# Layer 1 of a two-layer graph network: the score column is copied into PSUM by ScalarE and VectorE adds the row term in one operation, in place of one ScalarE add per chunk

## The chip, the cores and the metric

One Trainium2 chip, one of its cores. The metric is device time in microseconds (us) of one execution of the whole program. Engines are named as the profile names them: PE is TensorE, PEld its weight loads, DVE is VectorE, ACT is ScalarE, POOL is GpSimd, SP is SyncE; a "q" behind a name (SPq, PEq) is that engine's queue or sequencer.

## What is computed

There are 4096 nodes with 512 features and one adjacency matrix of about 0.8% density. Layer 0 is a normalised graph convolution with a residual; layer 1, which the change concerns, is graph attention with a positive and a negative softmax. Cut to what matters:

```python
def _L1_gnn_ref(inp, adj, W, a, wtrans):          # inp = relu(layernorm(x))
    h = inp @ W
    Wh1 = h @ a[:F_out, :]                        # one number per row: s
    Wh2 = h @ a[F_out:, :]                        # one number per column: t
    e = leaky_relu(Wh1 + Wh2.T, 0.2)
    mask = adj > 0
    attention = softmax(where(mask, e, NEG_INF), axis=1)
    negative_attention = -softmax(where(mask, -e, NEG_INF), axis=1)
    h_prime = attention @ inp
    h_prime_negative = negative_attention @ inp
    new_h_prime = concatenate([h_prime, h_prime_negative], axis=1) @ wtrans
    return elu(new_h_prime)
# x = x + _L1_gnn_ref(...)
```

## The kernel before, in words

Layer 0 is dense and takes about the first half of the time. While it runs, the kernel makes lists of the non-zero columns of every block of rows. Layer 1 is sparse: it works only on listed columns. The function that the change touches is `weights(r)` inside `sparse_layer1()`.

**Blocks and pairs.** The 4096 rows are 64 blocks `r` of `RB` = 64 rows; two blocks that follow each other are a pair (32 pairs). One pair is begun during layer 0 by other code (`early_pair`); the other 31 pairs, 62 blocks, go through the loop at the end of `sparse_layer1()`. In that loop pair 17 is first (blocks 34 and 35), then pair 20 (blocks 40 and 41), then 18, 19 and so on.

**Lists and gathers.** For every pair GpSimd gathers rows of a table into SBUF (`gather`, L506, one indirect DMA per chunk of 128 listed columns). A gathered row (`ROW` = 644 words) holds the 512 features, the column's score `t` (at `ROW_T` = 512) and the mask bytes (from `ROW_W` = 516). A pair has three gathered parts, `g0`, `g1`, `g2`, with `CHUNKS` = (8, 7, 7) chunks; one chunk of `g1` holds the pair's own rows, and SyncE brings it (`load_own`, L520). So a pair has 21 indirect gathers for its 22 chunks. The even block of a pair uses parts 0 and 1 (15 chunks), the odd one parts 1 and 2 (14 chunks). Two sets of the three buffers alternate between pairs.

**`weights(r)`**, for each of the block's two parts of n chunks, in the kernel before:

1. ScalarE, per chunk (L1765): `z[:, c] = s + t[:, c]`, an activation Identity over 128x64 whose bias is the chunk's column of `t`. `z` is a PSUM bank of its own; `s` is the block's row of scores, in SBUF.
2. ScalarE (L1767): `y = 0.2 z`, the whole part, to SBUF.
3. VectorE (L1768): `z = max(z, y)`.
4. ScalarE (L1773): `e = exp(z)` into a second PSUM bank, and `z = exp(-z)` in place.
5. VectorE, twice (L1777): mask `e` and `z` into `p` (SBUF), the weights of the block.

After both parts VectorE sums `p` over the chunks (L1787, `total`).

**`product(r)`**: TensorE sums `total` over partitions (L580, `cs`); VectorE takes the reciprocal (L585, `rl`) and a sign (L588); TensorE multiplies `p` with the gathered features (L556, `u`, 20 or 22 chunk products in two halves of 64 columns each); ScalarE scales `u` by `rl` into `us` (L1815). `turn(r)` transposes `us` on TensorE (L595, `tp`), and ScalarE copies it out (L602, `ut`). `project1` and `finish1` multiply `ut` by `wtrans` on TensorE (L1826, `o`), one half after an odd block, the other after an even one; VectorE and ScalarE apply the elu (L1843 to L1847, `eo`, `y`), and SyncE stores the rows.

**Order.** The loop body is: product of block k, gathers for later blocks, `weights` of block k+2, turn of block k-1, projection. Each engine runs its own instructions in order. The order is made by the tile framework's scheduler when the program is built, apart from a few instructions that are pinned (`keep_in_program_order`). PSUM has eight banks, and `bank(...)` hands them out in rotation, so an operation that writes a new bank waits for the last reader of the bank's previous tile.

**`scores(s, z, t)`** (L524 to L529) is a helper that `early_pair` uses already: one VectorE addition of `t` (broadcast over the 64 rows) and `s` (broadcast over the chunks).

Of the kernel before, what the change touches and what calls it, by code (L numbers as in the profile page):

```python
# [13 lines left out]
AF = mybir.ActivationFunctionType  # L14
# [18 lines left out]
RB = 64  # L33
# [240 lines left out]
def gcn_gat_kernel(  # L274
# [26 lines left out]
    nc = tc.nc  # L301
# [30 lines left out]
    def bank(name):  # L332
        return ps.tile([P, 512], F32, tag="ps", name=name)
# [4 lines left out]
    with sbuf(name="init", bufs=1) as init:  # L338
        column = init.tile([P, P], F32, name="column")
        nc.vector.memset(column[:, 0:1], 0.0)  # L340
        n = 1
# [182 lines left out]
    def scores(s, z, t):  # L524

        n = z.shape[1]
        return nc.vector.tensor_tensor(
            z, t.to_broadcast([P, n, RB]), s.unsqueeze(1).to_broadcast([P, n, RB]), ALU.add
        )  # L529
# [77 lines left out]
    with sbuf(name="y0", bufs=1) as y_pool, sbuf(name="wa", bufs=1) as wa_pool, sbuf(name="bits", bufs=4) as bits_pool, sbuf(name="small0", bufs=4) as small, ExitStack() as rest, ExitStack() as lists:  # L607
# [525 lines left out]
        i0, n = GROUPS[0]  # L1133
# [557 lines left out]
    def sparse_layer1():  # L1691
        nonlocal verdict
        with ExitStack() as pools:
# [55 lines left out]
            def parts(r):  # L1749

                t = [gath[r // 2][r % 2 + k] for k in range(2)]
                return (t[0], 0, t[0].shape[1]), (t[1], t[0].shape[1], t[1].shape[1])

            def weights(r):

                nk = sum(CHUNKS[r % 2 : r % 2 + 2])
                most = CHUNKS[0] + CHUNKS[1]
                p = p_pool.tile([P, most, 2, 2, SB], F32, tag="p", name=f"p{r}")[:, :nk]
                s = srow[r // 8][:, r % 8 * RB : (r % 8 + 1) * RB]

                for gt, k, n in parts(r):
                    z = bank(f"z{r}_{k}")[:, : n * RB].rearrange("p (k c) -> p k c", c=RB)
                    t = gt[:, :, ROW_T : ROW_T + 1].bitcast(F32)
                    for c in range(n):
                        nc.scalar.activation(z[:, c], s, AF.Identity, bias=t[:, c])  # L1765
                    y = tmp.tile([P, n, RB], F32, tag=f"y{n}", name=f"y{r}_{k}")
                    nc.scalar.activation(y, z, AF.Copy, scale=ALPHA)  # L1767
                    nc.vector.tensor_tensor(z, z, y, ALU.max)  # L1768
                    e = bank(f"e{r}_{k}")[:, : n * RB].rearrange("p (k c) -> p k c", c=RB)
                    mask = gt[:, :, ROW_W:].bitcast(U8)[:, :, r % RPT * RB : (r % RPT + 1) * RB]  # L1770
                    four = "p k (h i) -> p k h i"
                    for g, x in ((0, e), (1, z)):
                        i = nc.scalar.activation(x, z, AF.Exp, scale=(1.0, -1.0)[g])  # L1773
                        if r in first:
                            tc.keep_in_program_order(i)
                    for g, x in ((0, e), (1, z)):
                        nc.vector.scalar_tensor_tensor(  # L1777
                            p[:, k : k + n, :, g],
                            mask.rearrange(four, h=2),
                            0.0,  # L1780
                            x.rearrange(four, h=2),
                            ALU.is_gt,
                            ALU.mult,
                        )
                total = small.tile([P, 2 * RB], F32, tag="total", name=f"total{r}", bufs=3)
                q = p.rearrange("p k h g i -> p (h g i) k")
                nc.vector.tensor_reduce(total, q, AX.X, ALU.add)  # L1787
                for k in range(n_late if r in with_late else 0):
                    q = lates[r][:, k].rearrange("p h g i -> p (h g i)")
                    nc.vector.tensor_tensor(total, total, q, ALU.add)  # L1790
                wgt[r] = (p, total)
# [105 lines left out]
            load_wt(1)  # L1897

            weights(order[0])
            turns = [end0(n, small, work) for n in range(2)]  # L1900
            keep_late()
            weights(order[1])
            for k, r in enumerate(order):
                product(r)
# [10 lines left out]
                if k + 2 < len(order):  # L1915
                    weights(order[k + 2])
                    if wanted and order[k + 2] % 8 == 7:
                        load_s(wanted.pop(0))
# [66 lines left out]
```

## Time and profile before

| what | value |
|---|---|
| time, median of 6 runs (lowest to highest) | 2015.33 us (2008.39 to 2028.07) |
| the profiled execution: its own time / span of its trace | 2018.65 / 2016.9 us |
| granted TensorE clock, mean | 0.973 |
| layer 1's steady loop, about 1100 to 1950 us | 850 us of the span |
| the pair begun early and the first blocks, 960 to 1100 us | 140 us |
| the tail, 1950 to 2017 us | 67 us |
| L1765 over all | 812 + 87 activations, 0.32 us each |

How to read it: times are microseconds from the start of the span unless marked ns. In the group rows, "x" is the count, then busy time and mean ns of one, and behind the bar the idle time of that engine just before these instructions with what ended most of it ("issue": nothing that the profile shows). A timeline row is: start, duration, engine, line, operation, output<-inputs, sizes, count, and in brackets the idle time before it. The engines' busy shares are averages over stages with different limits, so layer 1 is read from its own stretches.

### The profile page before, as it was taken

How to read it: one execution, taken by the hardware profiler on the slowest of the kernel's cores; microseconds unless marked ns; L12 is line 12 of the kernel's file. 1: busy time of each engine (PE TensorE's matmuls, PEld its weight loads, DVE VectorE, ACT ScalarE, POOL GpSimd, SP SyncE). 2: the span in 40 equal slices, each digit the busy share in tenths (PEclk: the TensorE clock that was granted, in tenths of full speed). 3: DMA queues.
4: the chain of work that ended last, by engine and by line, in shares of the span. 5: the costliest groups of instructions: out<-in, count | busy, mean ns of one | idle time of the engine just before them, and what ended most of it. 6: DMA issues, size and time to landing. Idle time of an engine off the chain costs nothing.

```text
span 2016.9 us, 24509 instructions
## 1 busy us (share of the span) xinstructions
PE 1903.4 (94%) x7708; PEld 1058.3 (52%) x7708; DVE 1273.4 (63%) x2758; ACT 938.0 (47%) x2165; POOL 825.7 (41%) x919
## 2 busy tenths in 40 slices
PE   8999999999999999999879998989889899898998
PEld 3444468888888888884423333333333333333334
DVE  6766588898889979762625654545555455554552
ACT  6777743222223222221536655655555555564651
POOL 3110000034322233305555666666666666666640
PEclk9999999999999999999789999999999899999999
DMA  9999967576858586758867878887888787877860
GB/s 373 392 329 338 322 197 246 174 249 206 263 165 270 176 252 194 243 178 302 284 223 233 283 246 279 249 285 248 284 265 286 237 254 244 269 245 244 259 191 23
DMA packets 217218, 504.33 MB, mean 250 GB/s; under 512 B 35059, under 2 KB 69395, under 8 KB 217078
## 3 DMA queue, kind: packets, MB, share of 16 engines
q0 software_dynamic: 62560, 233.71, 36.2%
q1 hardware_dynamic: 114240, 236.49, 34.6%
q10 hardware_dynamic: 40278, 32.47, 5.2%
q8 instruction: 63, 1.03, 0.2%
q14 instruction: 77, 0.63, 0.1%
HBM read 457.77 MB, written 103.45 MB: 278 GB/s over the span
## 4 chain that ended last, share of the span: by engine, by line
PE 89%; issue 6%; DMA 2%; DVE 1%; ACT 1%; another core or an unknown queue 0%; ACTq 0%; DVEq 0%; SPq 0%
PE p L1105 31%; PE u L556 30%; PE o L1826 11%; PE acc L1064 5%; PE yp L890 5%; PE q L1465 3%; PE tp L595 2%; DMA ar<-in_adj 2%; PE counts L867 1%; PE cs L1541 1%; ACT z L1765 1%; PE tx L831 1%; PE o L1860 0%; PE cs L580 0%; DVE key L429 0%
## 5 line engine op out<-in xcount | busy, mean ns | idle before, releaser
L506 POOL DMA_INDIRECT g<-table,idx x672 | 641.6, 955 | 434.9 <-issue 177.5
L556 PE MATMUL u<-g,p 128*64 128x512 f32 x2604 | 622.3, 607 | 75.7 <-issue 75.1
L556 PEld LDWEIGHTS u<-g,p 128*64 128x64 f32 x2604 | 190.2, 138 | 445.7 <-issue 434.0
L442 POOL DMA_INDIRECT ld<-lst,off x160 | 144.7, 904 | 342.7 <-DMA ld<-lst,off 143.7
L1765 ACT ACTIVATE z<-s,g 128x64 f32<-128x64 f32 x812 | 259.4, 319 | 42.1 <-issue 10.9
L1105 PE MATMUL p<-y,at 128*128 128x256 f32 x832 | 248.0, 380 | 0.0
L1105 PE MATMUL p<-y,sums 128*128 128x256 f32 x832 | 247.4, 379 | 0.0
L1105 PE MATMUL p<-t,sums 128*128 128x256 f32 x832 | 245.5, 379 | 0.6 <-issue 0.6
L1826 PE MATMUL o<-wt,ut 128*128 128x512 f32 x496 | 235.3, 619 | 6.1 <-DVE total L1787 3.0
L1768 DVE TENSOR_TENSOR z<-z,y 128x512 f32<-128x512 f32 (+1 forms) x124 | 80.4, 648 | 204.3 <-ACT y L1767 91.3
L1787 DVE TENSOR_REDUCE total<-p 128x128 f32<-128x1920 f32 (+1 forms) x62 | 207.6, 3349 | 2.1
L1105 PEld LDWEIGHTS p<-t,sums 128*128 128x128 f32 x832 | 158.0, 190 | 22.7 <-issue 1.2
L1105 PEld LDWEIGHTS p<-y,sums 128*128 128x128 f32 x832 | 158.0, 190 | 21.5
L1105 PEld LDWEIGHTS p<-y,at 128*128 128x128 f32 x832 | 157.1, 190 | 23.2 <-issue 2.2
L1777 DVE SCALAR_TENSOR_TENSOR p<-g,z 128x512 f32<-128x512 uint8 (+1 forms) x124 | 78.4, 632 | 112.0 <-ACT z L1773 102.9
L1826 PEld LDWEIGHTS o<-wt,ut 128*128 128x128 f32 x496 | 94.8, 202 | 103.4 <-issue 98.5
L852 ACT ACTIVATE junk<-ar 128x1024 bf16<-128x1024 f32 x128 | 134.6, 1051 | 9.2 <-DMA ar<-in_adj 5.0
L930 ACT ACTIVATE m<-at 128x1024 uint8<-128x1024 f32 x110 | 113.0, 1047 | 51.9 <-DVE t_all L1032 16.0
L1773 ACT ACTIVATE e<-z 128x512 f32<-128x512 f32 (+1 forms) x124 | 67.1, 542 | 128.6 <-issue 71.3
L1777 DVE SCALAR_TENSOR_TENSOR p<-g,e 128x512 f32<-128x512 uint8 (+1 forms) x124 | 79.1, 638 | 74.4 <-issue 29.8
L1105 PE MATMUL p<-t,at 128*128 128x256 f32 x416 | 123.9, 380 | 1.2 <-DVE w L975 1.2
L1064 PE MATMUL acc<-y,at 128*128 128x512 f32 x256 | 120.3, 594 | 0.0
(220 smaller groups left out, 2037.1 us busy)
## 6 DMA issues: line engine op xcount, KB each, us to landing
ar<-in_adj SPq DMA_DIRECT2D x128, 512.0 KB
at<-in_adj_t SPq DMA_DIRECT2D x112, 512.0 KB
table<-table SPq DMA_DIRECT2D x49, 1032.0 KB
table<-m ACTq DMA_DIRECT2D x48, 256.0 KB
g<-table,idx POOLq DMA_INDIRECT x672
g<-table SPq DMA_DIRECT2D x32, 322.0 KB
at<-in_adj_t SPq DMA_DIRECT2D x32, 256.0 KB
xr<-in_x SPq DMA_DIRECT2D x32, 256.0 KB
```

The source lines that it names most:

```text
L442: return nc.gpsimd.indirect_dma_start(out=lst_dram[g][e % TURNS][:, :], out_offset=bass.IndirectOffsetOnAxis(ap=off[g][:, e, c : c + 1], a ...
L506: i = nc.gpsimd.indirect_dma_start(out=gt[:, k, :], out_offset=None, in_=table[2 * n // RPT], in_offset=bass.IndirectOffsetOnAxis(ap=idx[n ...
L556: i = nc.tensor.matmul(u[h * RB : (h + 1) * RB], p[:, k, h].rearrange("p g i -> p (g i)"), row(k), start=begin and k == HALVES[r % 2][h][0 ...
L852: nc.scalar.activation(junk, ar, AF.Identity, accum_out=parts[j][:, c : c + 1])
L890: nc.tensor.matmul(yp, hx_t[j][:, c * P : (c + 1) * P], w0_sb[:, c, :], start=c == 0, stop=c == FC - 1,)
L930: nc.scalar.activation(m, at, AF.Sign)
L1064: nc.tensor.matmul(a, at[:, 0, it * P : (it + 1) * P], y0[j], start=j == 0, stop=j == NJ - 1)
L1105: i = nc.tensor.matmul(out, left[:, x * P : (x + 1) * P], right, start=jp == 0 and first, stop=jp == NP - 1 and (final or not first),)
L1765: nc.scalar.activation(z[:, c], s, AF.Identity, bias=t[:, c])
L1777: nc.vector.scalar_tensor_tensor(p[:, k : k + n, :, g], mask.rearrange(four, h=2), 0.0, x.rearrange(four, h=2), ALU.is_gt, ALU.mult,)
L1787: nc.vector.tensor_reduce(total, q, AX.X, ALU.add)
L1826: i = nc.tensor.matmul(halves[j], uts[j][:, g, c, :], wts[g][:, c, :], start=g == 0 and c == 0, stop=g == 1 and c == FC - 1,)
```

## The change

For each part, ScalarE no longer adds `s` and `t` chunk by chunk. The bank `e` of the part is taken earlier; ScalarE copies the part's columns of `t` (n numbers per partition) into column 0 of each chunk of that bank, and VectorE's `scores` adds `s` to them, broadcast, into `z`: one operation for the part. `y`, the maximum, the exponentials and the masking are as they were.

```diff
                     z = bank(f"z{r}_{k}")[:, : n * RB].rearrange("p (k c) -> p k c", c=RB)
                     t = gt[:, :, ROW_T : ROW_T + 1].bitcast(F32)
-                    for c in range(n):
-                        nc.scalar.activation(z[:, c], s, AF.Identity, bias=t[:, c])
+                    e = bank(f"e{r}_{k}")[:, : n * RB].rearrange("p (k c) -> p k c", c=RB)
+                    nc.scalar.copy(e[:, :, 0:1], t)
+                    scores(s, z, e[:, :, 0:1])
                     y = tmp.tile([P, n, RB], F32, tag=f"y{n}", name=f"y{r}_{k}")
                     nc.scalar.activation(y, z, AF.Copy, scale=ALPHA)
                     nc.vector.tensor_tensor(z, z, y, ALU.max)
-                    e = bank(f"e{r}_{k}")[:, : n * RB].rearrange("p (k c) -> p k c", c=RB)
```

The helper that it calls:

```python
    def scores(s, z, t):
        n = z.shape[1]
        return nc.vector.tensor_tensor(
            z, t.to_broadcast([P, n, RB]), s.unsqueeze(1).to_broadcast([P, n, RB]), ALU.add
        )
```

Where the built program differs: TensorE's and GpSimd's instructions stand in the same order as before. On SyncE the load of `s` moves ahead of one `load_own` in five places. On ScalarE and VectorE the order within `weights` changes: ScalarE's copy for the second part of a block stands ahead of the first part's `y`, and a copy waits for all gathers of its part at once, where each activation of L1765 waited for its own chunk's. VectorE's additions stand behind the reciprocal L585 and, for odd blocks, among the operations of L1843 to L1847. In the after kernel the lines of `y` and of the maximum are one higher (L1768, L1769), the copy is L1765, and the addition carries the helper's L527.

## The prediction

> **What bounds the kernel now.** I read the page first (the chain of waits, then the groups), next a table by stage, then the timelines of the start of layer 1 and of one steady pair. From the page:
>
> ```profile
> PE 89%; issue 6%; DMA 2%; DVE 1%; ACT 1%; another core or an unknown queue 0%; ACTq 0%; DVEq 0%; SPq 0%
> ...
> L1765 ACT ACTIVATE z<-s,g 128x64 f32<-128x64 f32 x812 | 259.4, 319 | 42.1 <-issue 10.9
> ...
> L1768 DVE TENSOR_TENSOR z<-z,y 128x512 f32<-128x512 f32 (+1 forms) x124 | 80.4, 648 | 204.3 <-ACT y L1767 91.3
> ```
>
> The chain of waits is TensorE for 89% of the span. ScalarE's line of the change appears in it with 1%, about 20 us. The second row is the work that is removed: 319 ns each, and ScalarE sat idle before it for only 42 us in all, mostly not for gathers. The third row is the nearest one to the operation that is added: a VectorE addition with its output and one input in PSUM. The table by stage:
>
> ```profile
> core 0: us, PE busy (x) PEld busy (x) DVE busy (x) ACT busy (x) POOL busy (x), PEclk, DMA share, GB/s
> ...
> 1050.00:1100.00 50.00, 44.42 (x178) 16.48 (x174) 28.26 (x34) 29.15 (x80) 29.79 (x33) 0.97 0.75 241
> ...
> 1400.00:1600.00 200.00, 183.40 (x716) 69.50 (x714) 103.70 (x130) 114.67 (x308) 127.77 (x134) 0.97 0.83 270
> ```
>
> In a steady 200 us TensorE works 183, VectorE 104 and ScalarE 115. A pair of blocks takes about 31 us, so TensorE is idle for some 2.5 us per pair. The idle time that the chain shows there is runs of about 1.4 us with no releaser ("issue"), once in 31 to 34 us (1158, 1189, 1221, 1255, 1288 us), each time at a slightly different place of the block, so I take it for TensorE's own instruction stream and not for ScalarE. Two waits are of another kind. They lie in the start of layer 1; this is TensorE's timeline:
>
> ```profile
> 1038.12 11.80 PE L556 MATMUL u<-g,p 128*64 128x512 f32 x44 [7.30 <-issue]
> ...
> 1056.14 5.37 PE L1826 MATMUL o<-wt,ut 128*128 128x512 f32 x8 [3.04 <-DVE total L1787]
> ...
> 1070.89 3.60 PE L1826 MATMUL o<-wt,ut 128*128 128x512 f32 x8
> ...
> 1086.24 3.70 PE L1826 MATMUL o<-wt,ut 128*128 128x512 f32 x8 [1.35 <-DVE eo L1843]
> ```
>
> Before 1056.14 TensorE waited 3.04 us, and the eight projection products that follow took 5.37 us where the same eight take 3.60 and 3.70. Before 1086.24 it waited 1.35 us. The other two engines at the first wait:
>
> ```profile
> 1042.37 2.46 ACT L1765 ACTIVATE z<-s,g 128x64 f32<-128x64 f32 x7
> ...
> 1052.65 3.37 DVE L1787 TENSOR_REDUCE total<-p 128x128 f32<-128x1920 f32 x1
> ...
> 1055.93 0.15 DVE L585 RECIPROCAL rl<-cs 128x1 f32<-128x1 f32 x1
> ```
>
> ScalarE was blocked until 1040.74 by the evacuation of the first block (L1815), then did the additions of pair 20's first block, which put its `total` at 1052.65. The reciprocal for which TensorE waited stands behind that sum in VectorE's order.
>
> **What the change removes and adds.** It removes 812 + 87 = 899 ScalarE activations: 899 x 0.319 = 287 us. It adds 62 x 2 = 124 ScalarE copies of 7 or 8 elements. No such row exists; the nearest are the copy L1047 (2x128, 0.25 us) and the 128x1 activation L800 (0.20 us), so 25 to 31 us. ScalarE's 583 us in 900 to 2017 us fall by about 258 us. It adds 124 VectorE additions; by L1768 (0.694 us for 512 elements, 0.633 for 448) that is 31 x 0.694 + 93 x 0.633 = 80 us. VectorE's same addition from SBUF (L527, two parts in 1.22 us) is a little cheaper: 76 us. VectorE goes from 52% to 60% of a steady pair, ScalarE from 57% to about 30%.
>
> *In the steady loop* none of this is on the path; the cover is that the weights are made two blocks ahead. In the built program the first product of a block waits for VectorE's first masking operation of the next block, because a PSUM bank passes on there. So that operation is what may come late:
>
> ```profile
> 1398.83 0.62 DVE L1777 SCALAR_TENSOR_TENSOR p<-g,e 128x448 f32<-128x448 uint8 x1 [0.59 <-ACT e L1773]
> ...
> 1404.58 3.24 DVE L1787 TENSOR_REDUCE total<-p 128x128 f32<-128x1792 f32 x1
> ...
> 1407.70 7.94 PE L556 MATMUL u<-g,p 128*64 128x512 f32 x34
> ...
> 1412.84 0.69 DVE L1777 SCALAR_TENSOR_TENSOR p<-g,e 128x512 f32<-128x512 uint8 x1 [0.65 <-issue]
> ...
> 1413.19 2.42 ACT L1765 ACTIVATE z<-s,g 128x64 f32<-128x64 f32 x7
> ...
> 1424.50 9.66 PE L556 MATMUL u<-g,p 128*64 128x512 f32 x44
> ```
>
> Block 52 starts at 1407.70 and needs block 53's first mask, made at 1398.83 to 1399.45: a margin of 8.2 us. Block 53 starts at 1424.50 and needs block 54's, ended at 1413.53: 11.0 us. The change puts two additions (1.3 us), a copy (0.25) and about 0.7 of the other part's maximum ahead of that mask, and takes 7 x 0.35 = 2.4 us of activations away: between 2.3 us later and 0.2 us earlier, inside both margins. New waits: the copy for the second part needs all seven chunks and stands ahead of the first part's `y`. Behind it are queued that `y`, the exponentials, L1815 and L602, and for them TensorE's transposes. In the timeline the last of block 54's six second-part gathers was issued at 1407.69, and its last chunk was read at about 1414.9, so it landed between these. From there the copy, an addition, the way from `y` to the end of the mask (2.67 us from 1101.13 to 1103.80 in the same timeline further up) and the other part's maximum are 0.25 + 0.69 + 2.67 + 0.7 = 4.3 us: 1412 to 1419.2, still 5.3 us before 1424.50. The odd block's second part was issued by 1416.46 and was not read before 1430.40, so it is not late. For the moved SyncE load of `s`: it goes ahead of one own-row load, each 0.3 us of issue, and both are read a block later: nothing. POOL is not moved; it waits for TensorE to free its buffers. In the tail the last gather is issued at 1949.21, and TensorE is busy for 57 of the last 67 us: nothing.
>
> *At the start* the path does shorten. From 1042.37 to 1051.86 ScalarE spent 2.46 + 2.42 = 4.9 us on the fifteen additions. With the copy of the first part ahead of the blocked L1815, VectorE has added before 1040.74. `total` moves forward by 4.9 - 0.25 - 0.1 = about 4.5 us, to 1048.1, and ends at 1051.5. What is late next is TensorE itself: its sum over partitions for that reciprocal starts at 1051.57 and ends at 1051.95. So of the 3.04 us some 2.5 go. The slow products after the wait (5.37 against 3.60) are 1.8 us more if they are slow because TensorE had been idle. The 1.35 us at 1086 ended with VectorE's elu, which stands behind the next `total` (1081.52 to 1085) and moves forward by as much: gone. Sum: 2.5 + 1.8 + 1.35 = 5.6 us at most; at least 0, if TensorE meets a gather instead. I take 4.0, nearer to the upper end because each term is a row.
>
> The granted clock shows what hangs on idling: 0.88 and 0.78 in 950 to 1000 and 1000 to 1050 us, where TensorE worked 43 and 39 of 50 us, and 0.97 when it worked 44. By the row of 5.37 us the slow products belong to the wait, and go with it. [...]
>
> So: 2018.65 - 4.0 = 2014.6 for the profiled execution, which lay 3.3 us above the median. Against the median: **2011.3 us**. A measurement of this kernel can tell about 0.5%, 10 us, from no change.
>
> **Rivals.** *Nothing but the start moves* (the forecast): 2011 us, within 10 us either way. Chance 0.52.
>
> *Faster: the start's chain goes as a whole.* From 1040 to 1086 us the chain of waits runs through ScalarE. TensorE also waited 7.30 us before 1038.12, and that wait ended with the reciprocal at 1037.90, which the profile ascribes to no engine. If it moves with VectorE's earlier `total` of block 35, then 7.3 + 5.6 = 12.9 us go: 2015.3 - 12.9 = 2002. Against it: all that the reciprocal formally needs is a sum on TensorE, and the DMA engines moved 415 GB/s in 1025 to 1031 us, so the delay may be theirs. A ScalarE with 30% of work may also return fractions of a microsecond per pair that I read as TensorE's own; 0.3 us in 29 pairs would be 9 us more. Chance 0.29.
>
> *Slower: VectorE becomes late.* Place: the first mask of the next block. It decides from the point where the additions, the copy's wait for the whole part and VectorE's longest waits at the reciprocal (3 to 4.7 us) together exceed the 8.2 us margin. My own bound is 2.3 + 4.7 = 7.0. An addition that reads a broadcast from PSUM at twice the row's price adds 1.3 and crosses it by 0.1; with a late gather by perhaps 0.6 us per pair, 29 x 0.6 = 17 us: 2032. For it: VectorE's order now interleaves with the elu. Against it: the margins. Chance 0.19. That the change does not do what it says is excluded by the built program.
>
> **The numbers.** The forecast's own range is 2003 to 2020 (its 0 to 5.6 us, and 5 us either way for a median of runs that span 20 us). The whole range reaches down to the faster case and half of the way to the slower one: 2000 to 2026. Faster by over 0.5% (under 2005) 0.29, within 0.52, slower (over 2025) 0.19.
>
> **What would show it.** Right: 124 additions of 0.6 to 0.7 us under L527 in layer 1, copies near 0.22 us, ScalarE's busy time about 258 us lower, TensorE's gap at 1056 gone, and the same pitch of about 31 us per pair. Wrong: TensorE waiting at the first product of a block for VectorE's masks (slower), the steady pair shorter by more than 0.3 us (faster), or additions well over 0.7 us.

## The result and the profile after

Where the change was measured it made the kernel slower: 2045.19 us (median of 20 runs) against 2016.34 us (46 runs), ratio 1.0142, 95% interval 1.012 to 1.0163, some 29 us. The forecast was 2011.3 us. The profiled execution of the changed kernel took 2071.56 us (span 2069.8), 1.3% over its own median, so the differences between the two traces are larger than the 29 us; the joined runs shown below stand also in traces within 0.3% of their kernel's median (late_copy, direct_again).

The page of the kernel after, its chain of waits and the groups that stand in the place of L1765:

```profile
PE 82%; issue 8%; POOL 5%; DVE 2%; another core or an unknown queue 1%; DMA 1%; ACT 0%; POOLq 0%; DVEq 0%; ACTq 0%; SPq 0%
...
L1815 ACT ACTIVATE us<-u,rl 128x512 f32<-128x512 f32 x62 | 42.6, 687 | 361.1 <-remote 241.7
L527 DVE TENSOR_TENSOR z<-e,s 128x512 f32<-128x512 f32 (+1 forms) x112 | 71.4, 638 | 138.0 <-issue 97.2
```

The added operations cost what was forecast: 638 ns per addition (0.63 to 0.69 in the forecast), 0.18 us per copy (0.25). ScalarE's busy time fell from 938.0 to 675.4 us, 263 us (258). But TensorE's share of the chain fell from 89% to 82%; "issue" rose from 6% to 8%, and GpSimd's gathers appear in it with 5%. ScalarE now sits idle for 361 us before `us` (L1815), 242 us of it put down to "remote", which names no engine; what that is shows below. The table by stage:

```profile
core 0: us, PE busy (x) PEld busy (x) DVE busy (x) ACT busy (x) POOL busy (x), PEclk, DMA share, GB/s
1050.00:1100.00 50.00, 49.46 (x200) 17.81 (x198) 32.93 (x47) 16.66 (x45) 28.63 (x30) 0.96 0.69 215
1400.00:1600.00 200.00, 176.07 (x663) 67.39 (x660) 107.76 (x147) 56.26 (x136) 117.65 (x125) 0.91 0.78 254
```

In the same 200 us TensorE did 663 products, not 716; ScalarE was busy for 56 us instead of 115, VectorE for 108 instead of 104. Nothing is full, and the granted clock is 0.91 instead of 0.97. The loss is in TensorE's timeline, in the second block (44 products) of a pair (the row of 40 is its first block):

```profile
1277.72 8.80 PE L556 MATMUL u<-g,p 128*64 128x512 f32 x40
...
1290.59 1.30 PE L556 MATMUL u<-g,p 128*64 128x512 f32 x2
1294.11 0.59 PE L556 MATMUL u<-g,p 128*64 128x512 f32 x1 [2.22 <-issue]
1296.93 1.01 PE L556 MATMUL u<-g,p 128*64 128x512 f32 x1 [2.23 <-issue]
1298.34 1.01 PE L556 MATMUL u<-g,p 128*64 128x512 f32 x1 [0.40 <-issue]
1300.44 1.01 PE L556 MATMUL u<-g,p 128*64 128x512 f32 x1 [1.08 <-issue]
1301.83 1.01 PE L556 MATMUL u<-g,p 128*64 128x512 f32 x1 [0.38 <-issue]
1303.24 9.84 PE L556 MATMUL u<-g,p 128*64 128x512 f32 x37 [0.40 <-issue]
```

and in GpSimd's of the same time, where the gathers had followed each other at 1.25 us since 1273.46, 21 of them:

```profile
1298.47 0.95 POOL L506 DMA_INDIRECT g<-table,idx  x1 [0.30 <-issue]
1309.92 0.94 POOL L506 DMA_INDIRECT g<-table,idx  x1 [10.50 <-PE u L556]
```

From 1291 to 1297 us TensorE started one product or weight load per 1.4 us, then until 1303 us one per 0.7 to 1.4 us; four of the rows show products of 1.01 us, and the granted clock was 0.50 from 1297 to 1303 us. The gathers of the pair, which are to follow the block, then waited 10.5 us for it. TensorE is not alone in this. ScalarE and VectorE, in the same time:

```profile
1303.33 0.69 ACT L1815 ACTIVATE us<-u,rl 128x512 f32<-128x512 f32 x1 [15.13 <-remote]
...
1303.49 0.69 DVE L1843 TENSOR_SCALAR eo<-o 128x512 f32<-128x512 f32 x1 [10.82 <-remote]
```

This `us` belongs to the first block, whose products had ended at 1286.5 us, and the projection products ahead of the elu (L1843) had ended at 1290.5 us; both engines stood still until TensorE's slow stretch was over. So the 361 us are not all products that come late. The same two blocks' place in the kernel before:

```profile
1279.23 7.94 PE L556 MATMUL u<-g,p 128*64 128x512 f32 x34
1287.69 0.59 PE L556 MATMUL u<-g,p 128*64 128x512 f32 x1 [0.53 <-issue]
1290.48 1.60 PE L556 MATMUL u<-g,p 128*64 128x512 f32 x5 [2.20 <-issue]
```

```profile
1287.05 0.95 POOL L506 DMA_INDIRECT g<-table,idx  x1 [0.30 <-issue]
1290.93 0.95 POOL L506 DMA_INDIRECT g<-table,idx  x1 [2.93 <-remote]
```

There the slow stretch lies at the end of the first block (40 products) of each pair, lasts some 4 us, and GpSimd pauses 3.9 us between the thirteen gathers of `g1` and `g2` and the eight of the next `g0`. In both kernels a slow stretch ends, to about 1 us, when the last gather of the run has landed.

The eight refill a buffer that the first half of the first block reads last: by the kernel's order of products, the 20th of the 40, which here had started by 1283.2 us. The eight still waited until 1290.93 us, about when the last of the thirteen landed (1290.8). It is so in both kernels wherever the two runs stay apart: the eight start 18.7 to 19.0 us after the first of the thirteen, within 0.4 us of the last landing (one pair of `before` starts 1.5 us later), although the first block ends anywhere from 16.0 to 22.2 us after it. The eight go without a pause almost only where TensorE has got through that half block early; the figures stand under "Time or number of instructions?".

Pair by pair, from the first of a pair's eight gathers to the next pair's:

| kernel | 13 and 8 gathers apart | 13 + 8 joined | mean pair, 10th to 31st |
|---|---|---|---|
| before | 21 of 21 pairs, 30.6 to 33.5 us | none | 31.56 us |
| after | 10 of 21, 38.9 to 40.9 us (they follow a joined run) | 11 of 21, 28.2 us | 33.64 us |

From 1076 to 1262 us the changed kernel runs at 30.7 to 31.2 us per pair, where the kernel before took 30.8 to 33.8. From 1273 us on every second pair joins: 28.2 us, then some 39.6. The sum: 21 x (33.64 - 31.56) = 43.7 us in these pairs, 2.8 before them and 6.5 behind them, together 53 us, the difference of the two spans (2069.8 - 2016.9).

### The profile page after: what moved, and what is told of

It reads as the page before. It is cut to its first block, busy times and chain, and to the rows that moved or that the text cites. A ratio compares the mean times of both kernels' runs of the same rounds, so it can differ in the third digit from the quotient of the medians.

```text
span 2069.8 us, 23672 instructions
## 1 busy us (share of the span) xinstructions
PE 1919.7 (93%) x7708; PEld 1070.0 (52%) x7708; DVE 1331.3 (64%) x2882; ACT 675.4 (33%) x1390; POOL 824.2 (40%) x919
## 4 chain that ended last, share of the span: by engine, by line
PE 82%; issue 8%; POOL 5%; DVE 2%; another core or an unknown queue 1%; DMA 1%; ACT 0%; POOLq 0%; DVEq 0%; ACTq 0%; SPq 0%
PE p L1105 30%; PE u L556 26%; PE o L1826 9%; PE yp L890 5%; PE acc L1064 5%; POOL g L506 5%; PE q L1465 3%; PE tp L595 1%; PE counts L867 1%; DMA ar<-in_adj 1%; PE tx L831 1%; PE cs L1541 1%; PE o L1860 0%; DVE total L1787 0%
## 5 line engine op out<-in xcount | busy, mean ns | idle before, releaser
L556 PE MATMUL u<-g,p 128*64 128x512 f32 x2604 | 646.4, 624 | 81.4 <-issue 72.7
L556 PEld LDWEIGHTS u<-g,p 128*64 128x64 f32 x2604 | 207.9, 143 | 471.3 <-issue 454.2
L1815 ACT ACTIVATE us<-u,rl 128x512 f32<-128x512 f32 x62 | 42.6, 687 | 361.1 <-remote 241.7
L527 DVE TENSOR_TENSOR z<-e,s 128x512 f32<-128x512 f32 (+1 forms) x112 | 71.4, 638 | 138.0 <-issue 97.2
L1843 DVE TENSOR_SCALAR eo<-o 128x512 f32<-128x512 f32 x31 | 21.4, 691 | 165.7 <-remote 98.5
L890 PE MATMUL yp<-w_sb,hx_t 128*128 128x512 f32 x256 | 119.6, 611 | 0.7 <-DVE hx_t L836 0.7
L585 DVE RECIPROCAL rl<-cs 128x1 f32<-128x1 f32 x64 | 10.5, 164 | 147.3 <-PE cs L580 45.0
```

Source lines behind the costliest of these rows:

```text
L527: return nc.vector.tensor_tensor(z, t.to_broadcast([P, n, RB]), s.unsqueeze(1).to_broadcast([P, n, RB]), ALU.add)
L556: i = nc.tensor.matmul(u[h * RB : (h + 1) * RB], p[:, k, h].rearrange("p g i -> p (g i)"), row(k), start=begin and k == HALVES[r % 2][h][0 ...
L890: nc.tensor.matmul(yp, hx_t[j][:, c * P : (c + 1) * P], w0_sb[:, c, :], start=c == 0, stop=c == FC - 1,)
```

## The experiments

The kernels of one set ran on one chip, beside fresh runs of the kernel before. That kernel took 1859 to 1861 us (medians) in four sets and 1996 to 2021 us in the three others; 2016 us was the figure where the change was measured. The difference is the slow stretches: at 1860 us TensorE has no stretch of one instruction per 1.4 us. "With slow stretches" and "without" below mean this. The expectations speak of chips with and without them, but the record does not bear out that the chip decides: by its chip numbers, number 13 had none in the sets of after_again and of busy_long, and had them in the set of busy_act, which ran between the two. Three theories stood at first. A (A' once it was seen that only some sets have slow stretches): freed of its additions, ScalarE lets TensorE get so far ahead that two runs of gathers join, and the longer run makes a longer slow stretch. B: the copy, which waits for a whole part, blocks ScalarE's queue. C: VectorE's additions.

### Four kernels without slow stretches

**pause_after**, and **pause_before** with the same edit on the kernel before:

```diff
-            pad(1408)
+            idle = pad(1408)                 # a spare tile, 128x352
...
+                if a == 0 and not pin:
+                    for _ in range(10):
+                        tc.keep_in_program_order(nc.gpsimd.memset(idle, 0.0))
                 gather(gt, n, a, True)
```

> The changed kernel, with ten GpSimd memsets of 128x352 (by the memset of 128x384, 0.41 us, about 4 us in all) ahead of each pair's eight first gathers. Theory A (the run of gathers): in the changed kernel every second pair issues 13 + 8 = 21 gathers without the pause of 3.8 to 3.9 us that the kernel before always has behind its 13th, and TensorE then starts one instruction per 1.4 us until they have landed. With the pause forced there is no run of 21, no odd block longer than 13 us, a pair takes 31 to 32 us and the time comes back to 2016 us or under. Theory B (the copy's wait for a whole part stands at the head of ScalarE's queue) and theory C (VectorE's additions): nothing that they name is touched, 2045 us or, with the pause on top, more.

> The kernel before with the same ten memsets in the same place. Theory A: it pauses 3.8 to 4.0 us there anyway, in all its pairs, and the memsets fall into that pause: 2016 us, within 0.5%. If the memsets cost GpSimd time that the pairs need, it becomes slower by up to 4 us in each of 28 pairs, and then pause_after has to be read against this one. Theories B and C say nothing of it.

Measured: 1.0614 (1.0596 to 1.0632) and 1.0569 (1.0551 to 1.0586) against a kernel before of 1859 us. There were no slow stretches to take away, and the idling only made GpSimd the bound: 30.7 us per pair, where direct, beside it, needs 26.3 to 27 in most pairs (mean 26.9). The question stayed open; the two say that ten memsets add 4.5 us to the pause (5.73 against 1.25).

**wait_only**, on the kernel before:

```diff
+                    e = bank(f"e{r}_{k}")[:, : n * RB].rearrange("p (k c) -> p k c", c=RB)
+                    nc.scalar.copy(e[:, :, 0:1], t)
                     for c in range(n):
                         nc.scalar.activation(z[:, c], s, AF.Identity, bias=t[:, c])
...
-                    e = bank(f"e{r}_{k}")[:, : n * RB].rearrange("p (k c) -> p k c", c=RB)
```

> The kernel before with ScalarE's copy of a part's column added ahead of its own additions, which stay: the copy's wait for the whole part without VectorE's addition and without the work that is saved. The copied values are not used. Theory A: ScalarE is as busy as before, or 25 us busier, so TensorE does not get ahead of the gathers: no runs of 21, 2016 us within 0.7%. Theory B: the wait is there in full, about 2045 us with TensorE waiting in the odd block. Theory C: 2016 us.

Measured: 1.0159 (1.0142 to 1.0176). **direct**, on the changed kernel:

```diff
-                    nc.scalar.copy(e[:, :, 0:1], t)
-                    scores(s, z, e[:, :, 0:1])
+                    scores(s, z, t)
```

> The changed kernel without the copy: VectorE's addition reads the column in the gathered tile itself, so that the wait for the part stands in VectorE's queue and not in ScalarE's. Theory A: ScalarE is relieved as in the changed kernel, so the runs of 21 gathers come too and the time is 2035 to 2050 us. Theory B: ScalarE's queue no longer waits, and the time is back at 2016 us or under, unless VectorE's queue pays for it. Theory C: as the changed kernel, 2045 us.

Measured: 0.9966 (0.9954 to 0.9978). So without slow stretches the copy's wait is a real cost, and B is right about something. TensorE's waits by what it waited for, from 1100 to 1780 us, first in wait_only, then in direct:

```profile
PE u L556 <- DVE p L1778: 32.6, 5, 9.1
```

```profile
PE u L556 <- DVE p L1776: 6.3, 3, 2.7
```

(total us, times, longest). Whether B is what costs 29 us elsewhere was still to be seen.

### The changed kernel without slow stretches

**after_again** is the changed kernel, **before_again** the kernel before, both unedited.

> The changed kernel as it is, on the chip of this call. The kernel before took 2016 us where the change was measured and 1859 us beside the last four kernels, in which TensorE never started one instruction per 1.4 us. Theory A' (the loss hangs on those slow stretches of TensorE): on a chip without them the change costs nothing or gains, ratio 0.99 to 1.00, no odd block over 12.6 us; on a chip with them the ratio is 1.01 to 1.02 with runs of 21 gathers in every second pair. Theory B (the copy's wait for the whole part): the ratio is 1.014 or more on either, because wait_only was 1.016 on the chip without slow stretches.

> The kernel before as it is, for its trace on the chip of this call. Theory A': if it takes about 1860 us, its even blocks last 8.8 us and its pairs 26.6 us, against 12 to 15 us and 31 to 32 us in the trace of before. If it takes about 2016 us, they last what they lasted there. Theory B says nothing of it.

Measured: after_again 1862.83 us, 1.0016 (1.0001 to 1.0031); before_again 1858.35 us in one run. Two later repeats (after_third, after_fourth) gave 1.0008 (0.9992 to 1.0025) and 1.0018 (1.0003 to 1.0033). Without slow stretches the change costs 0.1 to 0.2%, so about 26 of the 29 us hang on them. What remains is two effects that nearly cancel. The start, in TensorE's timeline of before_again and of after_again:

```profile
1023.45 5.40 PE L1826 MATMUL o<-wt,ut 128*128 128x512 f32 x8 [2.60 <-DVE rl L585]
1038.23 3.60 PE L1826 MATMUL o<-wt,ut 128*128 128x512 f32 x8
1053.62 3.70 PE L1826 MATMUL o<-wt,ut 128*128 128x512 f32 x8 [1.40 <-DVE y L1846]
```

```profile
1020.73 3.70 PE L1826 MATMUL o<-wt,ut 128*128 128x512 f32 x8
1033.81 3.60 PE L1826 MATMUL o<-wt,ut 128*128 128x512 f32 x8
1047.64 3.60 PE L1826 MATMUL o<-wt,ut 128*128 128x512 f32 x8
```

The two waits and the slow products of the forecast are gone: the third group starts 6.0 us earlier, and by the same count of products TensorE is 6.5 us ahead at 1100 us. It gives that back here (ScalarE's timeline, then TensorE's, of after_again):

```profile
1285.16 0.17 ACT L1765 COPY e<-g 128x7 f32<-128x7 f32 x1 [17.00 <-DMA g<-table,idx]
1285.27 0.59 ACT L1768 ACTIVATE y<-z 128x512 f32<-128x512 f32 x1
```

```profile
1287.99 8.56 PE L556 MATMUL u<-g,p 128*64 128x512 f32 x26 [6.16 <-DVE p L1777]
```

The copy for the second part waited 17.0 us with the first part's `y` behind it, and TensorE waited 6.16 us for the first mask. There are four such waits, 13.6 us in all; before_again has four of 6.6 us in all, for another reason. They come at every third pair, behind SyncE's copies of table rows (L498, three DMAs issued in 1.95 us at 1258.06 us), with which the DMA engines are full (share 1.01 and 383 GB/s from 1260 to 1286 us, 0.90 and 294 from 1230 to 1257).

### The order of the copies, with slow stretches

**late_copy**, on the changed kernel:

```diff
-                    nc.scalar.copy(e[:, :, 0:1], t)
+                    i = nc.scalar.copy(e[:, :, 0:1], t)
+                    if k:
+                        tc.keep_in_program_order(i)
```

> The changed kernel with one thing pinned: ScalarE issues the copy of a block's second part behind the first part's exponentials, and not ahead of the first part's y. Theory B (the copy's wait for gathers that have not landed blocks ScalarE's queue): on a chip without TensorE's slow stretches the waits of 2.6 to 6.4 us at the first products of every third pair go, ratio to the kernel before 0.995 to 0.999; on a chip with slow stretches 1.00 to 1.01. Theory A' (a free ScalarE lets TensorE end its even block before the 13th gather): ScalarE is relieved as before, so on a chip with slow stretches the runs of 21 gathers come in every second pair and the ratio stays at 1.01 to 1.02; on one without, nothing changes, ratio 1.00.

**direct_again** is direct once more.

> The kernel direct (no copy, VectorE's addition reads the column in the gathered tile) once more, on the chip of this call. On a chip without slow stretches: 0.9966 again by both. On a chip with them, theory A': runs of 21 gathers, ratio 1.01 to 1.02; theory B: no wait in ScalarE's queue, 1.00 or under.

Measured: 1.0155 (1.0112 to 1.0198) and 1.0184 (1.0134 to 1.0234). With slow stretches it makes no difference where the wait for the part stands: B falls as the cause of the 29 us. Both have joined runs of 21: 6 and 12 of 21 pairs, mean pair 32.36 and 33.03 us.

### Is it ScalarE's relief? With slow stretches

**busy_act**, on late_copy: ScalarE as busy as before, and its results unused.

```diff
                     scores(s, z, e[:, :, 0:1])
+                    for c in range(n):
+                        i = nc.scalar.activation(idle[:, :RB], s, AF.Copy, scale=ALPHA)
+                        tc.keep_in_program_order(i)
```

> late_copy with ScalarE kept as busy as in the kernel before: behind each copy one 128x64 activation per chunk of s into a spare tile, 7 or 8 per part, whose results are not used. VectorE adds, ScalarE's copies wait for whole parts, only ScalarE's slack is taken away again. Theory A' (a free ScalarE lets TensorE end its even block before the 13th gather): on a chip with TensorE's slow stretches the runs of 21 gathers go, a pair takes 31 to 32 us and the ratio is 0.995 to 1.005, against 1.0155 of late_copy; on one without, 1.00 to 1.01. Theory B (the copy's wait) and theory C (VectorE's additions): the ratio stays at 1.01 to 1.02 on a chip with slow stretches.

**pause6_after** is pause_after with `range(6)`.

> The changed kernel with six GpSimd memsets in place of the ten of pause_after ahead of each pair's eight first gathers: by the 4.5 us that the ten added (pause of 5.73 against 1.25 us) these add 2.7, so that the pause is 3.9 us, what the kernel before has there on a chip with slow stretches. Theory A': there, no run of 21, each pair takes 30.8 to 31 us as in the changed kernel's undisturbed pairs, and the ratio is 0.98 to 0.99. Theories B and C: 1.014 or more. On a chip without slow stretches GpSimd sets the pair by both: 21 x 1.25 + 2.7 = 28.9 us against 26.6 to 27, ratio 1.02 to 1.04.

Measured: busy_act 0.9954 (0.9931 to 0.9978), no joined run; pause6_after 0.9921 (0.9896 to 0.9945). Useless work on ScalarE takes the loss away and more (late_copy, 1.0155, and busy_act stand in two sets, each against its own kernel before), so neither the copy's wait nor VectorE's additions are the loss: A's first step holds. Forcing the pause works too, though not as fully as expected (0.98 to 0.99): with 13 and 8 kept apart, 8 and the next 13 joined in five of 21 pairs, and first blocks of 13 to 23 us came instead.

### Time or number of instructions?

In the traces with slow stretches I measured each stretch's beginning from the first gather of its run (to the last TensorE instruction ahead of a gap of over 1.05 us between starts), and counted the recorded instructions of all engines in between. Medians:

| kernel | begins after | instructions, all engines | of them ScalarE's | early pairs of 21 | joined runs, 21 pairs | mean pair | ratio |
|---|---|---|---|---|---|---|---|
| before | 14.6 us | 195 | 43.5 | 0 | 0 | 31.56 us | 1 |
| after | 17.0 us | 193 | 19 | 11 | 11 | 33.64 us | 1.0142 |
| late_copy | 16.3 us | 188 | 18 | 10 | 6 | 32.36 us | 1.0155 |
| direct_again | 19.8 us | 198 | 9 | 9 | 12 | 33.03 us | 1.0184 |
| busy_act | 15.0 us | 193.5 | 34 | 1 | 0 | 31.23 us | 0.9954 |
| busy_long_2 | 15.7 us | 183.5 | 20 | 11 | 3 | 31.76 us | 0.9916 |
| count_dve_2 | 14.9 us | 190 | 18 | 1 | 0 | 31.16 us | 0.9963 |

An early pair is one whose 20th product, the last that reads `g0`, ended within 9.4 us of the first of the thirteen gathers (in the other pairs 9.8 to 11.7 us). 29 of the 32 joined runs are in early pairs. pause6_after has slow stretches too (begun after some 16.4 us and 185 instructions), but its memsets keep these runs apart. The ratios are of medians, and the other columns of one trace each (for busy_long_2 of an execution of 2020 us, where the median is 2004).

The time varies with the kernel, the number hardly: about 190. With 13 of 15 ScalarE instructions per block gone, the 190 are reached some 2 us later. One reading (A2) was that this decides: the half block is done before the slow stretch begins, GpSimd does not pause, and the slow stretch, now in the second block, lasts until 21 gathers have landed. It was set against ScalarE's time alone (A1).

**busy_long**, on late_copy (one activation of 1.38 us per part), and **count_dve**, on late_copy (0.06 us each, behind the block's sum):

```diff
                     scores(s, z, e[:, :, 0:1])
+                    i = nc.scalar.activation(
+                        idle.bitcast(U8).rearrange("p (k c) -> p k c", c=RB),
+                        s.unsqueeze(1).to_broadcast([P, 22, RB]), AF.Copy, scale=ALPHA)
+                    tc.keep_in_program_order(i)
```

```diff
                 wgt[r] = (p, total)
+                for _ in range(nk):
+                    tc.keep_in_program_order(nc.vector.memset(idle[:, 0:1], 0.0))
```

> late_copy with ScalarE delayed by few instructions in place of many: behind each copy one 128x1408 activation of s into a spare tile (about 1.5 us by the 0.53 us of 448 elements), not the 7 or 8 of busy_act (7.5 x 0.256 = 1.9 us). In all slow traces TensorE's slow stretch begins after a nearly constant number of instructions of all engines since the first gather of the run: median 195 in before, 193 in after, 188 in late_copy, 194 in busy_act, but 14.6, 17.0, 16.3 and 15.0 us. Theory A1 (ScalarE's time holds TensorE back): as busy_act, slow stretches 15 us into a run, ratio 0.995 to 1.00 where there are slow stretches. Theory A2 (the number of instructions sets when TensorE becomes slow, and the change took 13 of 15 additions per block out of that number): as late_copy, slow stretches 16 to 17.5 us into a run, runs of 21 gathers, ratio 1.01 to 1.02. Where there are none, 1.00 to 1.01 by both.

> late_copy with the number of instructions restored on another engine: 14 or 15 VectorE memsets of 128x1 per block behind the block's sum, some 0.06 us each, where VectorE has slack; ScalarE stays relieved. Theory A1: as late_copy, 1.01 to 1.02 where there are slow stretches, with runs of 21 gathers. Theory A2: slow stretches 14.5 to 15.5 us into a run at 190 to 200 instructions, no runs of 21, pairs of 31 to 32 us, ratio 0.99 to 1.003. Where there are none, 1.00 by both.

With them, **pause64_after** (pause6_after with `range((6, 4)[a])` for `a` < 2) and **after_third** (the changed kernel):

> pause6_after (six memsets ahead of the eight gathers of a pair) with four more ahead of its thirteen, since there the pause of 3.0 us fell to 1.25 in every fifth or sixth pair and the runs joined on that side. Theories A1 and A2: no run of 21 on either side, every pair 30.8 to 31 us, ratio 0.98 to 0.99 where there are slow stretches, against 0.992 of pause6_after; where there are none GpSimd sets the pair, 21 x 1.25 + 2.7 + 1.8 = 30.8 us against 26.6 to 27, ratio 1.06. Theories B and C (the copy's wait, VectorE's additions): over 1.01.

> The changed kernel as it is, as the measure for the other three of this call. Where there are slow stretches: ratio 1.01 to 1.02, runs of 21 gathers in every second or third pair, slow stretches 16 to 18 us into a run, by A1 and A2. Where there are none: 1.00.

This set met no slow stretches: 0.9946 (0.9924 to 0.9967), 1.0125 (1.01 to 1.0149), 1.0616 (1.0598 to 1.0634) and after_third's 1.0008. Nothing was decided, and the first two ran again, with slow stretches:

> busy_long once more (beside the last call the kernel before took 1861 us and TensorE had no slow stretches, so that its question stayed open). Where there are slow stretches, theory A1 (ScalarE's time): they begin 15 us into a run, no runs of 21 gathers, ratio 0.995 to 1.00. Theory A2 (the number of instructions): 16 to 17.5 us into a run, at 185 to 200 instructions, with runs of 21, ratio 1.01 to 1.02. Where there are none: 0.9946 again.

> count_dve once more. Without slow stretches it cost 1.2%, in waits of TensorE for VectorE's elu (y L1850, 21.6 us in five waits), so the trace decides here rather than the ratio. Where there are slow stretches, theory A1: they begin 16 to 17.5 us into a run, as in late_copy, and there are runs of 21. Theory A2: they begin 14.5 to 15.5 us into a run, at 185 to 200 instructions, and the runs stay at 13 and 8; ratio 0.99 to 1.012.

Measured: busy_long_2 0.9916 (0.9887 to 0.9945), count_dve_2 0.9963 (0.9937 to 0.9989). In count_dve_2, with ScalarE as free as in the changed kernel, the slow stretch is back where the kernel before has it (TensorE, then GpSimd):

```profile
1285.75 7.94 PE L556 MATMUL u<-g,p 128*64 128x512 f32 x35
1294.20 0.59 PE L556 MATMUL u<-g,p 128*64 128x512 f32 x1 [0.52 <-issue]
1296.32 1.79 PE L556 MATMUL u<-g,p 128*64 128x512 f32 x4 [1.52 <-issue]
```

```profile
1293.52 0.95 POOL L506 DMA_INDIRECT g<-table,idx  x1 [0.30 <-issue]
1297.45 0.94 POOL L506 DMA_INDIRECT g<-table,idx  x1 [2.99 <-remote]
```

So count_dve_2 came out as A2 expected, in place, number and ratio. That does not prove A2, for the memsets also hold TensorE back: without slow stretches count_dve cost 1.25%, with TensorE waiting 21.6 us in five waits for VectorE, and in count_dve_2 one pair of 21 was early where late_copy had ten. And busy_long_2 fits neither theory: A2 expected stretches that begin 16 to 17.5 us into a run and 1.01 to 1.02, A1 15 us, no joined run and 0.995 to 1.00; measured were 15.7 us, three joined runs and 0.9916. It has as many early pairs as the changed kernel, and eight of the eleven did not join. What the runs show is that with ScalarE relieved TensorE gets through the half block early and runs join, and that many small instructions put back on ScalarE (busy_act), or put on VectorE (count_dve_2), take both away. Whether the number of instructions decides where a stretch begins, and what kept the early pairs of busy_long_2 apart, stays open.

### Both pauses

**pause64_after_2** and **after_fourth** repeat the two kernels of those names.

> pause64_after once more, for a chip with slow stretches of TensorE. GpSimd's pairs are then held at 8.75 + 3.05 + 15.0 + 3.95 = 30.8 us on both sides, and no two runs of gathers can join, however early TensorE ends its blocks. If the joined runs are what the change loses by: every pair 30.7 to 31 us, no odd block over 13 us, 28 x (31.8 - 30.8) = 28 us less than the kernel before, ratio 0.98 to 0.99. If something else in the change costs time (the copy's wait, VectorE's additions), it stays and the ratio is 1.00 or more. Without slow stretches 1.06 again.

> The changed kernel as it is, as the measure on the same chip. With slow stretches: 1.01 to 1.02, slow stretches 16 to 18 us and 185 to 200 instructions into a run, joined runs of 21 in every second or third pair, and a pair joins where TensorE ends its even block less than 13.3 us after the first of the thirteen gathers. Without: 1.00.

No slow stretches again: 1.0614 (1.0592 to 1.0636) and 1.0018. Whether keeping the runs apart on both sides gains all of the 28 us where there are slow stretches was not measured.

No version was found that is both useful work and faster in both kinds of set. busy_long, with its idle activations, is (0.9946 and 0.9916); of the kernels without wasted work, direct gains without slow stretches (0.9966) and loses with them (1.0184).

## Why the prediction was wrong

**The step that failed** is in the reading of the steady loop: the runs of about 1.4 us "with no releaser" were taken for TensorE's own instruction stream "and not for ScalarE", and so left out of the sum. They recurred "once in 31 to 34 us", which is once per pair, and always near the end of a run of gathers. A stall that keeps step with the loop belongs to the loop. The runs showed that it hangs on the runs of gathers, near whose landing it ends, and on how far TensorE is ahead of them. With ScalarE relieved, TensorE ended the half block that frees `g0` 8.4 to 9.2 us after the first of the thirteen gathers in every second pair, where the kernel before needed 10.1 to 11.7 us in all. In those pairs two runs joined, and 4 us in each pair became some 11 us in every second one, with more time at half clock (mean granted clock 0.92 from 1100 to 1950 us, 0.96 before). Without slow stretches the change costs 0.1 to 0.2%, and with ScalarE kept busy the loss is gone (0.9954). What makes the engines stand still is not known. "POOL is not moved; it waits for TensorE to free its buffers" failed with it: in 11 of 21 pairs the eight gathers came 1.25 us behind the thirteenth and not 3.9.

**The removed and added work** was right: 263 us against 258 off ScalarE, additions of 0.638 us, copies of 0.18 us.

**The start** was right in its mechanism and a little short in size: 6.5 us without slow stretches, where the forecast had 5.6 at most and took 4.0. Where the change was measured the start can't be read: the same instructions stood up to 19 us apart at the fourth pair between executions of such kernels (1057 us in pause6_after, 1076 in after).

**The slow products** went with the wait. In before_again the wait was 2.60 us, the granted clock 0.72 from 1023 to 1029 us, and the eight products took 5.40 us; in after_again, without the wait, 1.00 and 3.70.

**The new wait** was named, its queue and its place were right, and its margin of 5.3 us was worked out on one pair. Pairs behind a table copy of SyncE's are others: there the copy waited up to 17.0 us and TensorE up to 6.16 us. That takes back the gain of the start, but it is not the 29 us.

**The rivals.** The slower one put its place at the first mask of the next block; TensorE does wait there, four times and 13.6 us in all, only where nothing else disturbs. It was not what decided the measurement. The faster one counted on the 7.30 us before 1038.12; in before_again the same 44 products (1008.35 us) follow without a wait, so that wait, too, was there only with slow stretches. The forecast's own range, by its terms, begins at 2004.7 us (2015.3 - 5.6 - 5) and not at 2003, which decides nothing.

## What to carry to other kernels

An idle time that no releaser explains but that keeps step with the loop is part of the loop: before it is left out of a sum, find out what it is in phase with, and ask what the change does to that. When a change removes many small instructions from an engine with slack, the ones that feel it may be the engines whose buffers come free earlier; look at which transfers then run into each other. And a margin is worked out on the worst pair, the one with the extra transfers, not on the one at hand.

## What was not expected of the hardware

- In some sets TensorE starts one instruction per 0.7 to 1.4 us, from about 190 recorded instructions (of all engines) into an unbroken run of gathers until they have landed, and ScalarE and VectorE stand still with it (15.13 and 10.82 us in the rows above); in others no such stretch comes in 244 gathers that start within 2 us of each other and 4276 instructions (before_again, 1484 to 1792 us). The same kernel takes 2016 and 1860 us there. What slows it there was not shown.
- The traces with slow stretches are themselves incomplete. They hold changes of semaphores, from which the releasers are inferred, beside the instructions: 2590 to 3071 between 1100 and 1750 us in the eight traces with slow stretches, 9763 to 11430 in the twelve without. Of ScalarE's 1876 signals on one semaphore `before` has 1003 and before_again all. So data are missing from the recording of the very executions in which engines stood still, and the releasers named there ("remote", "issue") are not to be relied on. That makes the recording a possible cause of the slow stretches; no run here shows that it is the cause, for every timed execution has a span and a granted clock, so none was without a recording.
- After a wait of only 2.60 us TensorE's granted clock was 0.72 from 1023 to 1029 us, and eight projection products took 5.40 us where later ones took 3.60 and 3.70 (before_again).
